# The last batch's norm ahead of the sum before it, and two spare products behind its transposition

## The chip, the cores and the metric

The kernel runs on one core of one Trainium2 chip. A core has five engines with a queue of instructions each: PE multiplies matrices (a weight load, PEld in the profile, and then a MATMUL that streams the other operand past the weights), DVE and ACT do elementwise work, POOL does elementwise work and starts some transfers, and SP starts transfers. Each engine takes its own instructions strictly in the order in which the program lists them and waits on semaphores for the others. PE writes its results to PSUM, of which this kernel uses eight banks; everything else lies in SBUF. The metric is the device time of one execution in microseconds (us). PE's clock can be halved for a while by the chip; the profile shows the share that was granted as PEclk.

## The reference, cut to what matters

Four stages follow one another on an input of 16 batches, each 256 by 256 in 32-bit floats: a per-batch expert adapter with a layer norm, an attention block with 16 heads and a feed-forward part, a conditional branch of small dense layers that ends in a layer norm, and one step of a stencil scheme. The change touches only the seam between the last two:

```python
y = x + out
mu = jnp.mean(y, axis=-1, keepdims=True)
var = jnp.mean((y - mu) ** 2, axis=-1, keepdims=True)
f = (y - mu) * jax.lax.rsqrt(var + EPS) * gamma + beta

Af = A_grid[None] * f[:, None]
Bf = B_grid[None] * f[:, None]
gradv_Af = _grad(Af[:, 0], 1) + _grad(Af[:, 1], 2)
gradvv_Bf = _grad2(Bf[:, 0], 1) + _grad2(Bf[:, 1], 2) \
    + _grad(_grad(Bf[:, 2], 2), 1) + _grad(_grad(Bf[:, 2], 1), 2)
df = -gradv_Af + gradvv_Bf * 0.5
out = jnp.maximum(f + df * dt[:, None, None], 0.0)
```

`_grad` and `_grad2` are first and second differences along one axis, with one-sided forms at the borders. All arithmetic is in 32-bit floats.

## The kernel before, in words

A batch is held as two chunks (`c`, or `k` where it is the contracted side) of 128 rows by 256 columns. Every stage of the chain is a Python generator over the 16 batches (`adapt`, `prepare`, `project`, `weigh`, `attend`, `enter`, `feed`, `end`, `step`). While the program is written, a planner, `Flow`, holds an estimated clock for each engine and picks which generator goes on next: the one with the earliest due time among those whose inputs are ready by the estimate. `flow.pe(1.6)` and the like advance these estimates; they emit nothing. What comes out is one fixed order of instructions for each engine. PSUM banks come from the planner too: `misc` takes the bank that was released longest ago by the estimates, of seven, and `free` gives it back.

So the batches overlap nearly everywhere: while one batch is in the stencil step, PE has attention or feed-forward work of the next. Only at the very end is there nothing to fill in. Just before its last sum the step of batch 14 (`b == B - 2`, line 1124) waits until the branch of batch 15 is written out; from there on the step is the only generator left, so that the end of batch 14's step and the whole step of batch 15 stand alone in program order.

The norm that ends the branch stage is split. `take_stats` (lines 413 to 426, called for the branch at line 1081) computes mean and variance on DVE and then 1/sqrt on POOL: `rs` in lines 421 and 422, and `nb` in lines 424 and 425. The step of a batch then begins with `normalized_affine` (line 443). For batches 0 to 14 it does the multiplication by gamma and the addition of beta on POOL. For batch 15 its `hurry` form is taken: four DVE instructions, chunk by chunk, lines 447 and 450. Line 447 needs the mean only, line 450 needs `rs`. The result overwrites `y` and is called `f`.

The step of one batch, in the order of the code:

- line 1102: four transposes of `f` on PE into a PSUM tile `e_t` (line 464 in the helper);
- line 1105: three DVE products of the transposed `f` with grids: `b2_`, `a1`, `b1_`, shown by the profile as e_b, e_a and e_b;
- lines 1109 and 1110: two POOL products of `f` with grids, `a0` and `b0`;
- lines 1116 and 1117: eight matmuls into `e_z`, which need `b2_` only; line 1121: DVE adds `e_z` to `a0`;
- lines 1133, 1149, 1139 and 1133 again: 32 matmuls into `e_d`: four with `b0`, sixteen with `a1` and `b1_`, eight narrow ones of 32 by 32 at the seam of the chunks, and four with `a0`;
- line 1165: DVE computes `o = e_d * dt + f`, for batch 15 in two halves; line 1169: ACT takes the maximum with zero; line 1171: SP starts the store.

The tiles of the step rotate through eight buffers, and a batch takes seven of them in the order `tmp`, `b2_`, `a1`, `b1_`, `a0`, `b0`, `o`.

Of the kernel before, what the change touches and what calls it, by code (L numbers as in the profile page):

```python
# [19 lines left out]
P = 128  # L20
B, S, D = 16, 256, 256
NC = S // P
# [148 lines left out]
def chain_kernel(ctx: ExitStack, tc: tile.TileContext, t: dict, out: bass.AP):  # L171
    nc = tc.nc
    ctx.enter_context(tc.manual_schedule())
    BANKS = 7
    flow = Flow(BANKS)
# [4 lines left out]
    def fixed(name, shape, dtype=F32, pool=const):  # L180
        return pool.tile(shape, dtype, name=name, tag=name)
# [14 lines left out]
    def misc(name, shape):  # L196
        numbers[name] = n = flow.take()
        return pp.tile(shape, F32, name=name, tag=f"m{n}")

    def free(name, at):  # L200

        flow.free_at[numbers.pop(name)] = at
        return at
# [67 lines left out]
    ident = fixed("ident", [P, P])  # L271
# [135 lines left out]
    b2, ln3_g, ln3_b = (rows_b[:, i * D : (i + 1) * D] for i in range(3))  # L407
    dt = rows_b[:, 3 * D :]
    w1_sr, w2_sr = w_sr[:, :NC, :], w_sr[:, NC:, :]
    a0_g, a1_g, b0_g, b1_g, b2_g, g_m, h_m = (grids[:, :, i * S : (i + 1) * S] for i in range(7))  # L410
# [17 lines left out]
    def normalized(dst, src, stat, first=False):  # L428
        mv, rs, nb = stat

        if first or max(flow.clock["DVE"], flow.clock["POOL"]) <= flow.clock["ACT"] + 0.3:
            for c in range(NC):
                nc.vector.tensor_scalar(
                    dst[:, c, :], src[:, c, :], mv[:, c, 0:1], rs[:, c : c + 1], ALU.subtract, ALU.mult
                )
            return flow.dve(0.65, flow.clock["POOL"])
        for c in range(NC):
            nc.scalar.activation(
                dst[:, c, :], src[:, c, :], AF.Identity, bias=nb[:, c : c + 1], scale=rs[:, c : c + 1]
            )  # L440
        return flow.act(0.97)

    def normalized_affine(dst, src, stat, gamma, beta, tmp, hurry=False):
        if hurry:
            mv, rs, _ = stat
            for c in range(NC):
                nc.vector.scalar_tensor_tensor(  # L447
                    tmp[:, c, :], src[:, c, :], mv[:, c, 0:1], gamma, ALU.subtract, ALU.mult
                )
                nc.vector.scalar_tensor_tensor(  # L450
                    dst[:, c, :], tmp[:, c, :], rs[:, c : c + 1], beta, ALU.mult, ALU.add
                )
            return flow.dve(2.1)
        at = normalized(tmp, src, stat)
        both = [P, NC, D]
        nc.gpsimd.tensor_tensor(tmp, tmp, gamma.unsqueeze(1).to_broadcast(both), ALU.mult)
        nc.gpsimd.tensor_tensor(dst, tmp, beta.unsqueeze(1).to_broadcast(both), ALU.add)
        return flow.pool(2.7, at)

    def transposed(ps, src):  # L460

        for k in range(NC):
            for c in range(NC):
                nc.tensor.transpose(  # L464
                    ps[:, k, c * P : (c + 1) * P], src[:, c, k * P : (k + 1) * P], ident
                )
        return flow.pe(0.44)
# [13 lines left out]
    ready, ys, stats2, lns, hts, stats3 = {}, {}, {}, {}, {}, {}  # L481
# [605 lines left out]
    def step():  # L1087
        def wide(name):
            return hp.tile([P, NC, S], F32, name=name, tag="g", bufs=8)

        yield lambda: ("branch", 0) in done
        for g in (a0_g, a1_g):
            nc.gpsimd.tensor_scalar(g, g, -1.0, None, ALU.mult)
        for b in range(B):
            yield lambda: ("branch", b) in done
            y, stat, at = stats3.pop(b)
            yield at, 0
            tmp = wide(f"e_tmp{b}")
            f = y
            yield normalized_affine(f, y, stat, ln3_g, ln3_b, tmp, b == B - 1)  # L1100
            ps_t = misc(f"e_t{b}", [P, NC, S])
            at = transposed(ps_t, f)
            b2_, a1, b1_ = (wide(f"e_{n}{b}") for n in ("b2", "a1", "b1"))
            for dst, grid in ((b2_, b2_g), (a1, a1_g), (b1_, b1_g)):
                nc.vector.tensor_tensor(dst, ps_t, grid, ALU.mult)  # L1105
                at = flow.dve(0.6, at)
            free(f"e_t{b}", at)
            a0, b0 = wide(f"e_a0{b}"), wide(f"e_b0{b}")
            nc.gpsimd.tensor_tensor(a0, f, a0_g, ALU.mult)
            nc.gpsimd.tensor_tensor(b0, f, b0_g, ALU.mult)  # L1110
            flow.pool(2.7)
            yield at - 1.4
            ps_z = misc(f"e_z{b}", [P, NC, S])
            for c in range(NC):
                rng = slice(c * P, (c + 1) * P)
                nc.tensor.matmul(ps_z[:, c, :], b2_[:, 0, rng], g_m[:, 0, :], start=True, stop=False)  # L1116
                nc.tensor.matmul(  # L1117
                    ps_z[:, c, reach[1]], b2_[:, 1, rng], g_m[:, 1, reach[1]], start=False, stop=True
                )
            at = flow.pe(1.35)  # L1120
            nc.vector.tensor_tensor(a0, ps_z, a0, ALU.add)
            at_z = free(f"e_z{b}", flow.dve(0.61, at))
            yield 0.0
            if b == B - 2:
                yield lambda: ("branch", B - 1) in done
            o = wide(f"e_o{b}")
            ps_d = misc(f"e_d{b}", [P, NC, S])

            def own(w, src, c, start=False, stop=False):
                rng = slice(c * P, (c + 1) * P)
                nc.tensor.matmul(ps_d[:, c, :], w[:, c, rng], src[:, c, :], start=start, stop=stop)  # L1133

            def next_to(w, src, c):
                near, far = slice(0, 32), slice(P - 32, P)
                at, of = (near, far) if c else (far, near)
                rng = slice(c * P + at.start, c * P + at.stop)
                nc.tensor.matmul(  # L1139
                    ps_d[at, c, :], w[of, 1 - c, rng], src[of, 1 - c, :], start=False, stop=False  # L1140
                )

            for c in range(NC):
                own(h_m, b0, c, start=c == 0)
            for c in range(NC):
                rng = slice(c * P, (c + 1) * P)
                for k in range(NC):
                    for src, w in ((a1, g_m), (b1_, h_m)):
                        nc.tensor.matmul(  # L1149
                            ps_d[:, c, reach[k]],  # L1150
                            src[:, k, rng],
                            w[:, k, reach[k]],
                            start=False,
                            stop=False,
                        )
            flow.pe(2.65)
            yield at_z
            for w, src in ((h_m, b0), (g_m, a0)):
                for c in range(NC):
                    next_to(w, src, c)  # L1160
            for c in range(NC):
                own(g_m, a0, c, stop=c == NC - 1)
            at = flow.pe(1.6)
            for part in [slice(c, c + 1) for c in range(NC)] if b == B - 1 else [slice(0, NC)]:
                nc.vector.scalar_tensor_tensor(  # L1165
                    o[:, part, :], ps_d[:, part, :], dt[:, b : b + 1], f[:, part, :], ALU.mult, ALU.add
                )
                at = flow.dve(0.75, at)
                nc.scalar.activation(o[:, part, :], o[:, part, :], AF.Relu)  # L1169
                flow.act(0.54, at)  # L1170
                nc.sync.dma_start(out=out[b].rearrange("(c p) d -> p c d", p=P)[:, part, :], in_=o[:, part, :])
            free(f"e_d{b}", at)
            done.add(("step", b))
# [7 lines left out]
    flow.add(feed(), 2.55, 13.9)  # L1181
    flow.add(end(), 3.08, 3.95)
    flow.add(step(), 4.65, 7.0)
    flow.run()

# [80 lines left out]
```

## Time and profile before

| what | value |
|---|---|
| time, median of 3 runs | 912.29 us (911.93 to 915.16) |
| the profiled execution's own time | 912.22 us |
| its span, first to last instruction shown | 910.4 us |
| PE busy in the span | 869.3 us (95%) |
| DVE, ACT, POOL busy | 636.2, 544.1, 377.4 us |
| mean granted PE clock | 0.99 |
| last matmul of batch 14 ends | 892.86 us |
| last matmul of the kernel ends | 906.24 us |

The profile is one execution, with times from the span's start. A row of its timeline gives a start, a length (from the first start to the last end if several instructions are merged), the engine, the source line, the operation with output and inputs, how many, and in square brackets how long the engine had been idle before and which instruction's end released it. A row of its windows gives, for a stretch of time, each engine's busy time with the number of instructions, then the granted PE clock, the busy share of the transfer engines and GB/s. Ends of matmuls are modelled, and times on POOL are rough.

### The profile page before, as it was taken

The numbers are of one execution on the slowest core, as the hardware profiler recorded it, in microseconds if no ns is written. First come the engines' busy times: TensorE is split into PE (matmuls) and PEld (weight loads), VectorE is DVE, ScalarE is ACT, GpSimd is POOL, SyncE is SP. The second block draws the span as 40 slices with busy tenths as digits, with TensorE's granted clock in tenths as the row PEclk, the third lists the DMA queues.
The fourth block names the chain that finished last, engine by engine and source line by source line (L and its number), as shares of the span: only waits on it lengthen the run. The fifth ranks groups of instructions, "written<-read, shape, count | busy, mean of one in ns | idle before, by whom it ended". The sixth has DMA issues, their size and how long they took to land. (4 is left out here: it accounts for less than half of the span.)

```text
span 910.4 us, 18249 instructions
## 1 busy us (share of the span) xinstructions
PE 869.3 (95%) x6184; PEld 668.7 (73%) x6184; DVE 636.2 (70%) x2087; ACT 544.1 (60%) x1537; POOL 377.4 (41%) x514
## 2 busy tenths in 40 slices
PE   7889998999999999999999999999999999999996
PEld 3557676777878777676877777787778778776875
DVE  5677867778777867757758686866768676767443
ACT  2576857576664767557765665847557474756230
POOL 3353455445416353351627245542446332422231
PEclk9999999999999999999999999999999999999998
DMA  8599977777888668778478777765857776670000
GB/s 274 166 267 316 285 166 191 183 200 191 203 204 201 179 166 221 217 185 209 125 191 222 179 193 175 190 166 161 195 152 181 180 203 173 176 190 31 13 30 23
DMA packets 130973, 163.25 MB, mean 179 GB/s; under 512 B 12714, under 2 KB 94780, under 8 KB 130876
## 3 DMA queue, kind: packets, MB, share of 16 engines
q0 software_dynamic: 31680, 62.92, 34.0%
q1 hardware_dynamic: 97920, 96.92, 33.5%
q10 hardware_dynamic: 1275, 2.19, 0.7%
q8 instruction: 52, 0.85, 0.4%
q14 instruction: 46, 0.37, 0.1%
HBM read 94.89 MB, written 4.19 MB: 109 GB/s over the span
## 5 line engine op out<-in xcount | busy, mean ns | idle before, releaser
L769 ACT ACTIVATE c_pr<-c_sc,c_mx 128x256 f32<-128x256 f32 x512 | 255.2, 500 | 207.5 <-DVE c_mx L758 203.9
L758 DVE CUSTOM_DVE_ANT_0 c_sc<-c_s,side 128x256 f32<-128x256 f32 x512 | 193.8, 417 | 35.7 <-PE c_s L740 20.2
L472 DVE COPY c_pts<-c_pt 128x512 f32<-128x512 f32 x206 | 137.0, 683 | 21.8 <-PE c_pt L464 21.2
L464 PE MATMUL c_pt<-ident,c_pr 128*128 128x128 f32 x1024 | 144.7, 278 | 7.4 <-ACT c_pr L769 3.6
L464 PEld LDWEIGHTS c_pt<-ident,c_pr 128*128 128x128 f32 x1024 | 114.3, 141 | 43.3 <-issue 14.5
L421 POOL TENSOR_SCALAR rs<-mv 128x2 f32<-128x2 f32 x64 | 14.2, 222 | 279.7 <-DVE mv L418 278.9
L924 PE MATMUL d_f<-d_ht,w 128*128 128x256 f32 x512 | 122.9, 383 | 4.0 <-DVE c_mx L758 2.2
L954 PE MATMUL d_o<-w,d_z 128*128 128x256 f32 x512 | 116.3, 381 | 0.1
L517 POOL DMA_DIRECT2D side<-neg x60 | 82.2, 1379 | 76.6 <-DMA side<-in_side 48.9
L924 PEld LDWEIGHTS d_f<-d_ht,w 128*128 128x128 f32 x512 | 92.7, 190 | 18.7 <-DVE c_mx L758 3.7
L954 PEld LDWEIGHTS d_o<-w,d_z 128*128 128x128 f32 x512 | 94.9, 190 | 14.5 <-issue 1.9
L769 ACT ACTIVATION_READ_ACCUMULATOR c_pr<-c_sc,c_mx 128x1 f32 x512 | 96.2, 188 | 0.0
L740 PE MATMUL c_s<-c_kt,c_qz 32*128 32x256 f32 x1024 | 77.6, 401 | 4.8 <-DVE x L582 1.9
L823 PE MATMUL c_c<-c_pts,c_va 128*32 128x256 f32 x1024 | 74.1, 386 | 2.7 <-DVE c_pts L472 2.5
L740 PEld LDWEIGHTS c_s<-c_kt,c_qz 32*128 32x128 f32 x1024 | 48.9, 184 | 24.5 <-issue 9.7
L962 DVE SCALAR_TENSOR_TENSOR y<-d_o,y 128x256 f32<-128x256 f32 x32 | 13.6, 425 | 63.3 <-PE d_o L954 63.3
L823 PEld LDWEIGHTS c_c<-c_pts,c_va 128*32 128x32 f32 x1024 | 27.9, 109 | 36.9 <-issue 17.9
L943 ACT ACTIVATE d_f<-d_z 128x512 f32<-128x512 f32 x64 | 38.3, 598 | 27.0 <-DVE d_z L940 26.3
L940 DVE TENSOR_SCALAR d_z<-d_f,cols 128x256 f32<-128x256 f32 x94 | 41.0, 477 | 16.2 <-PE d_f L924 16.0
L422 POOL TENSOR_TENSOR rs<-rs,inv_sqrt 128x2 f32<-128x2 f32 x64 | 45.9, 717 | 5.3
L947 DVE SCALAR_TENSOR_TENSOR d_z<-d_f,d_z 128x512 f32<-128x512 f32 x64 | 43.4, 677 | 1.8 <-ACT d_f L943 1.8
L1029 POOL TENSOR_TENSOR y<-y,d_bout 128x256 f32<-128x256 f32 x32 | 23.6, 790 | 47.1 <-PE d_t L464 32.1
(156 smaller groups left out, 1539.7 us busy)
## 6 DMA issues: line engine op xcount, KB each, us to landing
side<-in_side SPq DMA_DIRECT2D x256, 256.0 KB, 5.3
side<-neg POOLq DMA_DIRECT2D x60, 1024.0 KB, 8.1
d_w<-in_W_branch SPq DMA_DIRECT2D x16, 512.0 KB, 4.4
xt<-in_x_t SPq DMA_DIRECT2D x16, 256.0 KB, 6.1
x<-in_x SPq DMA_DIRECT2D x16, 256.0 KB, 5.9
out<-e_o SPq DMA_DIRECT2D x15, 256.0 KB, 3.7
w<-in_W SPq DMA_DIRECT2D x2, 1024.0 KB, 7.5
d_bout<-in_bl_branch SPq DMA_DIRECT2D x16, 128.0 KB, 4.5
```

The costliest lines, as they stand in the source:

```text
L422: nc.gpsimd.tensor_tensor(rs, rs, inv_sqrt, ALU.pow)
L464: nc.tensor.transpose(ps[:, k, c * P : (c + 1) * P], src[:, c, k * P : (k + 1) * P], ident)
L472: nc.vector.tensor_copy(dst, ps)
L517: nc.gpsimd.dma_start(out=sides[m].rearrange("p (h c) k -> p h (c k)", h=HB), in_=negs[m // 4].rearrange("p c k -> p (c k)").unsqueeze(1). ...
L740: nc.tensor.matmul(ps[i][:, c, :], qz[rows32, par, half, c * P : (c + 1) * P], k_t[rows32, half, :], start=b > 0, stop=b > 0 or c == NC - 1,)
L758: nc.vector.tensor_tensor_reduce(out=sc[:, c, :], in0=ps[i][:, c, :], in1=sb[:, i * NC + c, :], scale=-1.0, scalar=3.0e38, op0=ALU.add, op ...
L769: nc.scalar.activation(pr[:, c, :], sc[:, c, :], AF.Exp, bias=mx[:, c : c + 1], scale=-1.0, accum_out=sums[:, c, h : h + 1],)
L823: nc.tensor.matmul(ps_c[32 * i : 32 * i + 32, :], va[:, k, 4 * half + i, 2 * par : 2 * par + 2, :].rearrange("p e d -> p (e d)"), turned[i ...
L924: nc.tensor.matmul(ps_f[:, i, :], w1[:, k, f * P : (f + 1) * P], h_t[:, k, :], start=k == 0, stop=k == NC - 1,)
L940: nc.vector.tensor_scalar(z[:, i, :], ps_f[:, i, :], b1[:, f : f + 1], None, ALU.add)
L947: nc.vector.scalar_tensor_tensor(z, ps_f, 1.0, z, ALU.add, ALU.mult)
L954: nc.tensor.matmul(ps_o, us[f // 2][:, f % 2, c * P : (c + 1) * P], w2[:, f, :], start=f == 0, stop=f == NF - 1,)
```

## The change

For batch 15 the call of `normalized_affine` in its `hurry` form moves. It stood at the head of that batch's step; now it stands in the step of batch 14, behind that step's last matmuls and ahead of its DVE sum of line 1165. The four DVE instructions are the same. The head of batch 15's step only takes up the result. Its `tmp` tile is still requested between batch 14's `o` and batch 15's `b2_`, so every buffer's place in the rotation stays. Behind batch 15's four transposes, two matmuls are added: the identity as weights against 256 columns of a grid that has been in SBUF for long, into a PSUM bank taken for them that nobody reads. Other batches are written as before.

```diff
+        last = []
+
+        def awake(*columns):
+
+            ps = misc("awake", [P, NC * S])
+            for n in columns:
+                nc.tensor.matmul(ps[:, :n], ident, b2_g[:, 0, :n], start=True, stop=True)
+            free("awake", flow.clock["PE"])
+
         yield lambda: ("branch", 0) in done
         for g in (a0_g, a1_g):
             nc.gpsimd.tensor_scalar(g, g, -1.0, None, ALU.mult)
         for b in range(B):
             yield lambda: ("branch", b) in done
-            y, stat, at = stats3.pop(b)
-            yield at, 0
-            tmp = wide(f"e_tmp{b}")
-            f = y
-            yield normalized_affine(f, y, stat, ln3_g, ln3_b, tmp, b == B - 1)
+            if b < B - 1:
+                y, stat, at = stats3.pop(b)
+                yield at, 0
+                yield normalized_affine(y, y, stat, ln3_g, ln3_b, wide(f"e_tmp{b}"))
+                f = y
+            else:
+                f, at = last.pop()
+                yield at
             ps_t = misc(f"e_t{b}", [P, NC, S])
             at = transposed(ps_t, f)
+            if b == B - 1:
+                awake(256, 256)
...
             for c in range(NC):
                 own(g_m, a0, c, stop=c == NC - 1)
             at = flow.pe(1.6)
+            if b == B - 2:
+                y, stat, at_y = stats3.pop(B - 1)
+                last.append(
+                    (y, normalized_affine(y, y, stat, ln3_g, ln3_b, wide(f"e_tmp{B - 1}"), True))
+                )
             for part in [slice(c, c + 1) for c in range(NC)] if b == B - 1 else [slice(0, NC)]:
                 nc.vector.scalar_tensor_tensor(
                     o[:, part, :], ps_d[:, part, :], dt[:, b : b + 1], f[:, part, :], ALU.mult, ALU.add
```

## The prediction

> **What bounds the kernel now.** First the page's head: over the span PE is the busy engine.
>
> ```profile
> span 910.4 us, 18249 instructions
> PE 869.3 (95%) x6184; PEld 668.7 (73%) x6184; DVE 636.2 (70%) x2087; ACT 544.1 (60%) x1537; POOL 377.4 (41%) x514
> ```
>
> But the change touches only the last 20 us, and there the bound must be read anew. The view for that is the chain that ended last, in order of time (start, length, what):
>
> ```profile
> 891.78 1.07 PE e_d L1133 x4
> 892.88 0.75 DVE e_o L1165
> 893.64 0.40 DVE e_tmp L447
> 895.59 0.56 PE e_t L464 x3
> 896.18 0.70 DVE e_b L1105
> 896.92 1.22 PE e_z L1116 x2
> 905.16 1.07 PE e_d L1133 x4
> ```
>
> From the end of batch 14's last matmul (892.86) the end is set by batch 15 alone: sum, norm, transposition, product on DVE, and then PE without a break to 906.24. For 4.06 us PE has only four transposes. What releases what is in the timeline of the same stretch (start, length, engine, line):
>
> ```profile
> 889.98 0.18 DVE L418 BATCH_NORM_AGGREGATE mv<-st 128x2 f32<-128x6 f32 x1
> 890.55 0.71 POOL L422 TENSOR_TENSOR rs<-rs,inv_sqrt 128x2 f32<-128x2 f32 x1
> 892.88 0.75 DVE L1165 SCALAR_TENSOR_TENSOR e_o<-e_d,rows_b,y 128x512 f32<-128x512 f32 x1 [2.72 <-PE e_d L1133]
> 893.55 0.48 DVE L447 SCALAR_TENSOR_TENSOR e_tmp<-y,mv,rows_b 128x256 f32<-128x256 f32 x1
> 895.05 0.48 DVE L450 SCALAR_TENSOR_TENSOR y<-e_tmp,rs,rows_b 128x256 f32<-128x256 f32 x1
> 896.91 1.26 POOL L1110 TENSOR_TENSOR e_b<-y,grids 128x512 f32<-128x512 f32 x1
> ```
>
> The statistics are complete on POOL at 891.26, and DVE stands idle for 2.72 us up to 892.88, in front of a sum that waits for PE; the norm stands behind that sum.
>
> Last the windows, for the clock (after the first pair of numbers PE's busy time; the granted clock is the third number from the right). Up to the last matmul the clock changes only at 15.69, 19.10, 36.17, 39.58, 66.89, 70.30, 896.32 and 903.15, and the spaces between are whole multiples of 3.413 us (36.17 to 66.89 is 9 of them, 66.89 to 896.32 is 243): a grid, so I asked for the windows of that grid:
>
> ```profile
> 12.28:15.69 3.41, 2.19 (x21) 1.78 (x18) 2.02 (x8) 1.21 (x2) 1.84 (x2) 1.00 1.01 373
> 882.67:886.08 3.41, 1.99 (x8) 1.44 (x8) 0.21 (x1) 1.31 (x3) 1.22 (x2) 1.00 0.00 0
> 892.91:896.32 3.41, 0.85 (x4) 0.45 (x4) 2.63 (x6) 0.63 (x1) 0.64 (x1) 1.00 0.21 77
> 896.32:899.73 3.41, 2.81 (x9) 2.45 (x10) 1.74 (x3) 0.00 (x0) 1.85 (x2) 0.50 0.00 0
> 899.73:903.15 3.42, 3.42 (x14) 3.06 (x14) 0.69 (x1) 0.00 (x0) 0.00 (x0) 0.50 0.00 0
> ```
>
> The window with only the four transposes is followed by half clock; the next, with 2.81 busy, does not lift it; the full one after it does, at 903.15. So the gap costs twice: its length, and a stretch of 6.83 us at half speed behind it.
>
> **Part 1, the norm's new place.** Nothing is removed: four DVE instructions move ahead of one. No transfer is among them, and SP's and POOL's orders stay. The first (L447) needs the mean, there at 890.16. The second (L450) needs rs at 891.26, so I start it at 891.32. The next three distances are those of before (0.40, 0.52, and 0.48 for the last one's length): 891.72, 892.24, done at 892.72. New is that batch 14's sum, its ReLU and its store, and the three products of batch 15 now queue behind a wait for POOL. The sum waits for PE until 892.86 anyway, so that wait is covered by 0.14 us; beyond that each us of lateness of rs is a us on the path. The buffers asked for: tmp takes the one of batch 13's output, whose store was issued some 40 us before. I cost this at nothing.
>
> **Part 2, where the stall goes.** The last three transposes take 0.55 us; with y ready at 892.72 plus the 0.06 of before they run from 892.78 to 893.33. Late next is DVE: the sum stays at 892.88, and the instruction behind it started 0.67 later in the trace, at 893.55. So the first product (L1105) starts at 893.57 instead of 896.18, and e_z, 0.74 behind it as before, at 894.31 instead of 896.92: **2.61 us**. That is more than the norm's own 1.98, because the transposes also go under the sum. After e_z comes b0 from POOL: L1109 starts 0.15 after y (892.87), L1110 1.23 later, ends 895.36; PE wants it at 895.70. Spare 0.34, no cost; both multiply in the company of DVE before as after.
>
> **Part 3, the two spare matmuls.** No row shows them; the nearest is L1133 with the same 128x256 (four in 1.07, the last with its drain: 0.21 each). Two are 0.43, from 893.35 to 893.78 plus a drain of some 0.2, in front of an instruction that waits until 894.31. Cost between 0 and 0.43, the latter if transposes came 0.5 late; below zero not by time, only by the clock. I take 0. Their bank is the one released longest ago in the plan, not the e_d of batch 14 that is still being read.
>
> **Part 4, the clock.** Between 892.86 and 894.31 PE now has the transposes and 0.43 of full-width products; every window of 3.41 us that holds this stretch is otherwise full, so it has at least 3.41 - 1.45 + 0.43 = 2.39 us of dense matmuls. The window of 882.67, with eight such matmuls and 1.99 busy, kept full clock. The 2.19 of the window from 12.28, which lost it, is mostly sixteen products of 16 columns and says little of dense ones. So I expect full clock to the end. The work from e_z on then costs what batch 14's did: e_z from 880.61 to 881.92, the next group's start, 1.31, plus 0.08 for the first after a wait; e_d from 887.99 to 892.86, 4.87. Together 6.26 against 9.32 (896.92 to 906.24): **3.06 us**.
>
> Here the Trainium skill has a rule that speaks against my sum ("TensorE: Matmul & The Clock Gate", Part 1): the window runs free and does not restart with the kernel. The row agrees as to the grid (243 windows without drift), but one trace cannot show another phase. By the row, 3.06 are saved. By the rule, the stretch at half clock lies differently in each run of before. If the clock falls just after 896.92, the window behind is full, it lasts 3.41 and costs 1.7; if it falls before that, two windows may be needed, 2.3 to 3.3. The sum would then be anywhere from 4.3 to 5.9. The same page's Part 4 says that transpose mode does not count as PE being busy; the 892.91 window, which had nothing but transposes, fits, and I counted none above.
>
> **Sum.** Last matmul 894.31 + 6.26 = 900.57 instead of 906.24. The tail behind it stays: half sums, ReLU, store, 4.16 to the span's end, and 1.82 outside it. 912.22 - 2.61 - 3.06 = 906.55 for the profiled execution; the median of 912.29 stands 0.07 above it: 906.6. Because this trace's phase is near the dear end of what the clock can cost, I set 0.2 back: **906.8 us**.
>
> **The rivals.** (a) *The clock falls all the same*, because the products with the identity and the short gap are not enough. For it: the 2.19 window. Against: the 1.99 one. Only the 2.61 remain: 909.7. (b) *The start of e_z does not move that far*: POOL's products come late, since POOL's times are rough. For it: b0 is needed 2.6 us sooner and L1110 has 0.34 spare. If they take 1.5 longer, some 1.2 are lost, and 908 stands. (c) *Slower*: line 450 waits for rs ahead of batch 14's sum, with every later DVE instruction behind. The price is a us for each us that POOL ends after about 891.4; from 5.7 late the gain is gone, from 10.3 late it is 0.5% slower, 917. The row gives POOL nothing else in these 8 us, so this is hardly more than a formality. (d) *The change does not do what it says*: the first norm instruction is held until PE is through with batch 14 by a buffer or a wait that before's trace can't show, and nothing moves; 912.3. Against it: the tmp buffer is long free, and y has no reader left.
>
> **How the numbers follow.** About 0.5% (4.6 us) is what a measurement of this kernel can tell from no change. Full clock and moved start together: 0.86, own range 905.6 to 908; of these 0.70 are beyond 907.7 downwards, 0.16 are runs in which the half clock had cost before less than 2 us. (a) 0.07, (b) 0.02, (d) 0.02, all same; (c) 0.03. So faster 0.70, same 0.27, slower 0.03. The range is 905.6 to 909.9: from the largest sum with some early half-clock stretches shorter, to case (a).
>
> **What would show it.** Right: L447 near 890.2, L450's last end before 892.9, batch 14's L1165 still directly behind PE's last matmul; first L1105 some 0.7 behind that; e_z less than 1.6 behind batch 14's last matmul; two matmuls into the new bank between; granted clock 1.00 in all windows after it; from e_z to the last matmul about 6.3. Wrong: a clock of 0.50 after e_z, a wait of L1133 for POOL's L1110, or L1165 of batch 14 released by L450 and not by PE. The forecast fails most easily by the phase: if before's median runs had paid only 1.7 for the clock, 908 comes out with every step right.

## The result, and the profile after

The changed kernel took 907.80 us in the median of 6 runs (906.92 to 909.53), beside 912.13 (910.42 to 915.16) for the kernel before. The ratio is 0.9943 with a 95% interval of 0.9924 to 0.9962, 5.2 us or 0.57% faster (from 3.5 to 6.9 us). The ratio is an estimate over the single executions and not the quotient of the two medians, which lie 4.3 us apart. On another chip, beside other runs, the same kernel gave 907.76 and 0.9945 (0.9927 to 0.9964). The profiled execution took 907.62 us, with a span of 905.8.

Its timeline around the end of batch 14 (start, length, engine, line, in brackets the idle time before and its releaser; the change has moved lines 1105, 1116, 1133 and 1165 to 1119, 1130, 1147 and 1184):

```profile
891.15 0.45 DVE L447 SCALAR_TENSOR_TENSOR e_tmp<-y,mv,rows_b 128x256 f32<-128x256 f32 x1
891.32 0.36 POOL L421 TENSOR_SCALAR rs<-mv 128x2 f32<-128x2 f32 x1 [6.35 <-DVE mv L418]
891.76 0.71 POOL L422 TENSOR_TENSOR rs<-rs,inv_sqrt 128x2 f32<-128x2 f32 x1
892.51 0.51 DVE L450 SCALAR_TENSOR_TENSOR y<-e_tmp,rs,rows_b 128x256 f32<-128x256 f32 x1 [0.91 <-POOL rs L422]
893.45 0.48 DVE L450 SCALAR_TENSOR_TENSOR y<-e_tmp,rs,rows_b 128x256 f32<-128x256 f32 x1
893.75 0.79 PE L464 MATMUL e_t<-ident,y 128*128 128x128 f32 x4
893.96 0.75 DVE L1184 SCALAR_TENSOR_TENSOR e_o<-e_d,rows_b,y 128x512 f32<-128x512 f32 x1
894.37 1.03 PE L1097 MATMUL awake<-grids,ident 128*128 128x256 f32 x4
894.62 0.68 DVE L1119 TENSOR_TENSOR e_b<-e_t,grids 128x512 f32<-128x512 f32 x1
895.31 1.27 POOL L1124 TENSOR_TENSOR e_b<-y,grids 128x512 f32<-128x512 f32 x1
895.36 0.70 PE L1130 MATMUL e_z<-grids,e_b 128*128 128x256 f32 x2
```

The norm now runs while PE still works on batch 14, whose last matmul ends at 893.91 here. The transposes follow it at once, the sum of batch 14 runs beside them, and e_z starts 1.45 behind batch 14's last matmul, where it had been 4.06. In the windows of the clock's grid (in this execution its edges lie at 893.90 and every 3.413 us from there; PE's busy time is the second number, the granted clock the third from the right) the stretch that had lost the clock is full:

```profile
890.49:893.90 3.41, 3.41 (x26) 2.37 (x24) 2.40 (x7) 0.00 (x0) 1.54 (x4) 1.00 0.00 0
893.90:897.31 3.41, 3.41 (x20) 2.76 (x19) 2.85 (x6) 0.63 (x1) 2.50 (x2) 1.00 0.22 77
897.31:900.73 3.42, 3.42 (x28) 2.63 (x27) 0.42 (x1) 0.00 (x0) 0.00 (x0) 1.00 0.00 0
```

The chain that ended last, in order of time, has no DVE row left between the two batches. Its first e_d row behind e_z took 1.71 before (the first row here is from before) and takes 0.86 now:

```profile
899.86 1.71 PE e_d L1133 x4
```

```profile
893.92 0.62 PE e_t L464 x4
894.54 0.86 PE awake L1097 x4
895.40 0.65 PE e_z L1130 x2
896.93 0.86 PE e_d L1147 x4
900.57 1.07 PE e_d L1147 x4
```

The last matmul ends at 901.63, 6.27 behind e_z's start.

### The profile page after: what moved, and what is told of

Same layout as the page of the kernel before. It is cut to its first block, busy times and chain, and to the rows that moved or that the text cites. A ratio compares the mean times of both kernels' runs of the same rounds, so it can differ in the third digit from the quotient of the medians.

```text
span 905.8 us, 18259 instructions
## 1 busy us (share of the span) xinstructions
PE 867.4 (96%) x6188; PEld 668.2 (74%) x6188; DVE 636.7 (70%) x2087; ACT 544.1 (60%) x1537; POOL 377.6 (42%) x514
## 5 line engine op out<-in xcount | busy, mean ns | idle before, releaser
L421 POOL TENSOR_SCALAR rs<-mv 128x2 f32<-128x2 f32 x64 | 14.4, 224 | 281.4 <-DVE mv L418 280.5
L962 DVE SCALAR_TENSOR_TENSOR y<-d_o,y 128x256 f32<-128x256 f32 x32 | 13.6, 425 | 63.3 <-PE d_o L954 63.3
L947 DVE SCALAR_TENSOR_TENSOR d_z<-d_f,d_z 128x512 f32<-128x512 f32 x64 | 43.4, 678 | 1.8 <-ACT d_f L943 1.8
```

What stands on the lines that cost most here:

```text
L947: nc.vector.scalar_tensor_tensor(z, ps_f, 1.0, z, ALU.add, ALU.mult)
```

## The experiments

Two theories stood against each other on the clock: that the shorter gap alone keeps it, or that the two spare products do. A third question was whether rs is now what everything waits for, and what is left of the gap. The times beside each other were taken on one chip; "before" is the median of the kernel before there.

| run | median us | before | ratio (95% interval) |
|---|---|---|---|
| norm_alone | 908.42 | 913.12 | 0.9949 (0.9929 to 0.9969) |
| products_alone | 912.18 | 913.12 | 0.9981 (0.9967 to 0.9995) |
| products_filled | 910.68 | 913.12 | 0.9970 (0.9959 to 0.9981) |
| rs_late | 910.62 | 913.12 | 0.9980 (0.9971 to 0.9990) |
| after_again | 907.76 | 912.79 | 0.9945 (0.9927 to 0.9964) |
| late_one | 908.23 | 912.79 | 0.9939 (0.9916 to 0.9963) |
| late_one_bare | 909.94 | 912.79 | 0.9965 (0.9955 to 0.9974) |
| sooner | 907.48 | 912.79 | 0.9937 (0.9922 to 0.9953) |
| sooner_packed | 907.16 | 912.67 | 0.9934 (0.9913 to 0.9956) |

The medians hide most of what there is to see, because executions differ by several us before the end begins. So each profile is also cut at the start of batch 15's d_y matmuls (886.16 in before), the last point that all kernels share. "Half clock" adds up (1 - clock) x 2 x length over windows of 2 us ahead of that point; the last columns are distances in us from batch 14's last matmul to e_z, from e_z to the last matmul, and from d_y to the end of the span. They are taken from the ends as the profile holds them, and can differ by 0.02 from what its rounded rows give; the span is read to 0.1.

| profile of | d_y starts | half clock before it | gap to e_z | e_z to last | d_y to span end |
|---|---|---|---|---|---|
| before | 886.16 | 10.3 | 4.08 | 9.30 | 24.24 |
| before_look | 886.09 | 10.2 | 4.08 | 9.24 | 24.21 |
| after | 887.23 | 13.6 | 1.44 | 6.27 | 18.57 |
| after_again | 886.47 | 6.8 | 1.44 | 6.27 | 18.63 |
| norm_alone | 890.81 | 23.8 | 1.44 | 6.27 | 18.59 |
| norm_alone_b | 890.46 | 17.1 | 1.44 | 6.27 | 18.64 |
| norm_alone_c | 892.05 | 20.4 | 1.44 | 6.27 | 18.65 |
| products_alone | 886.75 | 13.6 | 4.94 | 6.90 | 22.75 |
| products_filled | 890.11 | 17.0 | 4.07 | 6.27 | 21.29 |
| rs_late | 886.16 | 10.2 | 4.23 | 7.37 | 22.54 |
| late_one | 887.40 | 17.0 | 2.50 | 6.28 | 19.70 |
| late_one_bare | 890.61 | 23.8 | 2.50 | 6.28 | 19.69 |
| sooner | 887.03 | 10.3 | none | 7.44 | 18.57 |
| sooner_packed | 890.23 | 17.1 | none | 6.27 | 17.57 |

The last column repeats within 0.1 us for one kernel; the first differs by 6 us over these executions, and mostly grows with the half clock ahead of it.

**The norm alone.** The change without its spare products:

```diff
-            if b == B - 1:
-                awake(256, 256)
```

> The norm is moved as in the change, the two spare products are left out. Behind batch 14's last matmul PE then has only four transposes in about 1.45 us before e_z, the rest of every 3.41 us window is dense. Theory (the moved norm does it, and the gap is now too short for the clock to fall): e_z still 1.45 behind batch 14's last matmul, granted clock 1.00 from there on, 6.3 us from e_z to the last matmul, time as with the whole change, 907.8 within 0.5. Rival (the spare products hold the clock): the same 1.45, but a clock of 0.50 behind it and 8 to 9.5 us from e_z to the last matmul, 909.5 to 911.

> The moved norm without the spare products, for another phase. Theory (a gap of 1.45 us is short enough in any phase): e_z to the last matmul 6.27 at full clock. Rival (the spare products are needed in some phases): a clock of 0.50 behind e_z and 7.5 to 9.5 us, in at least one of the two looks.

> The same once more, for a third phase: 6.27 us at full clock by the theory, 7.5 to 9.5 by the rival.

All three traces gave 1.44 and 6.27 at full clock, and from d_y to the span's end 18.59 to 18.65, where the change has 18.57 and 18.63. The median, 908.42, lies within its noise of the whole change. So in these traces the norm's new place does by itself all that the change does, the clock included. The chain of the third has DVE's product in the place of the spare ones, and e_z starts no earlier and no later:

```profile
898.78 0.75 DVE e_o L1175
899.53 0.61 DVE e_b L1110
900.18 0.70 PE e_z L1121 x2
```

The grid's edges, counted from d_y, lay nearly alike in the three traces (d_y at 0.67 to 0.72 of a window), so they are not three phases. In the third, the window that holds most of the gap was this:

```profile
896.60:900.01 3.41, 2.76 (x17) 1.49 (x16) 2.63 (x5) 0.45 (x1) 2.26 (x4) 1.00 0.00 0
```

Of the 1.44 us PE idles 0.81, so that no phase can leave a window with less than 2.6. In these traces the spare products neither saved nor cost anything. That they do nothing in any other phase is argued from the 2.6, not shown: with d_y at 0.05 of a window, as in the first trace of the change, the whole gap lies in one window, and the norm alone was not traced there. Nor is busy time by itself a sure measure. In products_filled the window from 14.05, mostly products of 16 columns, lost the clock with 2.56 busy, and in after_again the one from 30.89 kept it with 1.59.

**The products alone.** The norm stays in its old place, the two spare products are added behind the transposes:

```diff
             at = transposed(ps_t, f)
+            if b == B - 1:
+                awake(256, 256)
```

> The norm stays where it was before, the two spare products alone are added behind the transposes of batch 15. They run in a wait of 0.8 us and take 0.86 (four MATMUL records of 0.21 for two calls, as the trace after shows). Theory: the gap behind batch 14's last matmul stays at 4.06 us, a 3.41 us window in it has at most some 1.4 us of matmuls, the clock falls all the same; time as before, 912.1 within 0.7, e_z at most 0.1 later. Rival (the products are what lifts the clock): e_z 4.1 behind batch 14's last matmul as before, but full clock and 6.3 us from there, 909.0 to 909.8.

Its timeline:

```profile
896.66 1.91 PE L1095 MATMUL awake<-grids,ident 128*128 128x256 f32 x4
896.91 0.69 DVE L1114 TENSOR_TENSOR e_b<-e_t,grids 128x512 f32<-128x512 f32 x1 [0.79 <-PE e_t L464]
898.37 1.06 PE L1125 MATMUL e_z<-grids,e_b 128*128 128x256 f32 x2
```

The clock had fallen at 896.44, ahead of the products, so they took 1.91 instead of 1.03, and e_z waited for them: the gap is 4.94, not the "at most 0.1 later" that was expected. On the other hand they filled the window 896.44 to 899.85 (3.41 busy), and the clock came back after one window, not two: e_z to last 6.90. Together 1.5 us less than before in this trace. The median says 0.2% with an interval that ends just short of 1, below what counts as a change here. Both theories missed this mixture. In this trace the products alone did not keep the clock; other phases of the grid were not met.

**The clock alone.** The norm in its old place, and PE's waits filled with spare products:

```diff
+            if b == B - 1:
+                awake(256, 256, 256, 256)
...
-            at = transposed(ps_t, f)
+            at = transposed(ps_t, f, (lambda: awake(256)) if b == B - 1 else None)
+            if b == B - 1:
+                awake(256, 256)
```

The function handed to `transposed` is called between the first transpose and the second.

> The norm stays where it was before; the waits of PE between batch 14's last matmul and batch 15's e_z are filled with spare products: four calls (1.72 us) ahead of the transposes, one (0.43) between the first and the second transpose, two (0.86) behind them. This takes away the fall of the clock alone. Theory: e_z stays 4.06 to 4.2 behind batch 14's last matmul, granted clock 1.00, 6.3 us from e_z to the last matmul; saves what the clock costs, on average over the phase of the grid 2.3, at most 3.3: 909.0 to 910.4. Rival (the clock costs nothing on the median run, the norm's place is all): 912 within 0.5.

The gap stayed 4.07, and e_z to last went to 6.27 at full clock; d_y to the span's end is 2.95 shorter than in before. The ratio 0.9970 says 2.7 us (1.7 to 3.8), the medians 2.4. So of the change's 5.2 (5.67 in the traces) the clock by itself is worth about 2.7 (2.95), and the rest is the shorter gap.

**rs later.** The whole change, with two products of 128x512 on POOL ahead of batch 15's power:

```diff
+        if name == f"3_{B - 1}":
...
+            for _ in range(2):
+                nc.gpsimd.tensor_tensor(spare, b0_g, b1_g, ALU.mult)
         nc.gpsimd.tensor_tensor(rs, rs, inv_sqrt, ALU.pow)
```

> The whole change, with two extra products of 128x512 on POOL (1.27 us each by the neighbouring rows) ahead of the power that gives rs of batch 15; they go into a buffer that nobody reads any more. Theory: rs is on the path with no slack left, so the norm, the sum of batch 14, the transposes and e_z come 2.5 us later, and e_z stands 3.9 to 4.0 behind batch 14's last matmul. Of that gap PE has 1.5 us of work, so the clock falls in part of the runs: 907.8 plus 2.5 if it stays, plus 4 to 5.5 if it falls, 910.3 to 913. Rival (rs had slack, the sum of batch 14 or the transposes end last): less than 2.0 later, below 909.8.

The timeline and the window with the gap:

```profile
893.88 0.51 DVE L454 SCALAR_TENSOR_TENSOR y<-e_tmp,rs,rows_b 128x256 f32<-128x256 f32 x1 [3.34 <-POOL rs L426]
895.75 1.54 PE L1101 MATMUL awake<-grids,ident 128*128 128x256 f32 x4
897.08 1.06 PE L1134 MATMUL e_z<-grids,e_b 128*128 128x256 f32 x2
```

```profile
892.71:896.12 3.41, 1.20 (x7) 0.87 (x7) 2.21 (x5) 0.12 (x1) 2.26 (x5) 1.00 0.00 0
896.12:899.53 3.41, 3.41 (x12) 2.76 (x11) 1.71 (x3) 0.51 (x1) 1.83 (x2) 0.50 0.21 77
```

The gap is 4.23, a window with 1.20 busy cost the clock, and the whole is 4.0 longer from d_y than the change. The gap was expected at 3.9 to 4.0. The rest comes from the spare products: they took 1.54 here, most of it at half clock, and e_z waited for them, since the DVE product that it reads was done at 896.64. The median is 2.9 above that of the change on another chip, within what was expected. rs had no slack left.

**One late, with and without the products.** The same with one POOL product, once on the whole change, once on the norm alone.

> The whole change with one extra POOL product (1.27 us) ahead of the power of batch 15, so that the gap from batch 14's last matmul to e_z is some 2.7 us with four transposes and the two spare products in it. Theory (the clock goes by how much PE worked in a window of 3.41 us, and rows of 1.7 to 2.0 us held it): the window has some 1.6 us of matmuls and 0.6 of transposes, at the edge; full clock in the trace if it holds, and then 1.3 behind the change, 909; up to 3 more if it falls. Rival (spare products do nothing for the clock): same times with and without them.

> The same gap of some 2.7 us without the spare products: in it PE has four transposes only, so a window of 3.41 us that holds the gap has 0.7 us of matmuls. Theory: the clock falls to 0.50 behind the gap in nearly all phases, e_z to the last matmul takes 8 to 9.5 us in the trace, 1.7 to 3.3 slower than with the spare products, 911 to 912.5. Rival (the gap is still too short for the clock to fall, spare products or not): 6.3 us, 909.

Both gave a gap of 2.50, 1.06 longer than the change, and both kept full clock in the profile. Without the products it was this:

```profile
895.10:898.52 3.42, 2.55 (x16) 1.23 (x14) 1.50 (x4) 0.00 (x0) 2.32 (x4) 1.00 0.00 0
898.52:901.93 3.41, 2.63 (x15) 2.21 (x16) 2.87 (x5) 0.63 (x1) 2.50 (x2) 1.00 0.22 77
```

An edge of the grid cuts the gap in two, and each window keeps over 2.5 us of work. The expectation that the clock falls "in nearly all phases" without the products failed in this trace, and its median, 909.94, is below the 911 that was expected. By the ratios late_one_bare is slower than late_one by 0.26% of 912.8, 2.4 us (1.7 by the medians), with intervals that just overlap. That would fit a clock that the products hold in part of the runs at this longer gap, but the profile of late_one_bare also had 6.8 us more of half clock far ahead of the end than that of late_one. What the products do at 2.5 us stays open. Nor do the medians show late_one's longer gap: with four executions its 0.9939 is no higher than the 0.9945 of the change, though the trace has 1.1 us more from d_y to the end.

**What is left of the gap.** A version that goes on from the norm alone. Its core:

```diff
+            nc.vector.tensor_scalar(rs, mv[:, :, 1], EPS, None, ALU.add)
+            nc.gpsimd.tensor_tensor(rs, rs, inv_sqrt, ALU.pow)
...
             for c in range(NC):
                 nc.vector.scalar_tensor_tensor(
                     tmp[:, c, :], src[:, c, :], mv[:, c, 0:1], gamma, ALU.subtract, ALU.mult
                 )
+            for c in range(NC):
                 nc.vector.scalar_tensor_tensor(
                     dst[:, c, :], tmp[:, c, :], rs[:, c : c + 1], beta, ALU.mult, ALU.add
                 )
...
+                    heads.append(turned_grids(B - 1, y))
                 for c in range(NC):
                     own(g_m, a0, c, stop=c == NC - 1)
...
+            if b == B - 1:
+                for c in range(NC):
+                    for w, src in ((h_m, b0), (g_m, a0)):
+                        next_to(w, src, c)
+                    own(g_m, a0, c, stop=True)
```

`turned_grids` holds the transposes and the three products of line 1105; for batch 15 it now stands ahead of batch 14's last four MATMUL records.

> A version that goes on from the change, without spare products. For batch 15: epsilon is added on DVE, so that POOL has only the power to do; the two L447 instructions go ahead of the two L450 and fill the wait for it; the four transposes and the three DVE products go ahead of the last four MATMUL records of batch 14 and of its sum, so that these records fill PE's wait for the first product; the last e_d is in two tiles, chunk 0 ends before chunk 1's last products, and its sum, ReLU and store go under them. Theory (the rest of the gap is the power, the transposes and the first product in a row): y ready 0.9 us sooner, e_z about 0.6 behind batch 14's last matmul where it was 1.45, the tail behind the last matmul 0.4 shorter, full clock: 1.2 us below the change. Rival (POOL's b0 for batch 15, which waits for batch 14's last matmul, ends last): PE waits ahead of the e_d products, 0.4 to 0.6 below the change.

> The changed kernel as it is, on the chip of the runs beside it, to be compared with them and as a second look at another phase of the clock's grid. Both theories (spare products needed or not): e_z 1.45 behind batch 14's last matmul, full clock, 6.3 us from e_z to the last matmul, 0.5 to 0.65% below before.

e_z now follows batch 14's last matmul without a gap, 7.45 behind d_y where the change has 8.13, so 0.68 sooner. But nothing was gained: from d_y to the span's end 18.57, as the change. The rival's wait for POOL's b0 was not there either. The chain shows where it went: the narrow matmuls of line 1155 stand in it twice,

```profile
898.71 0.97 PE e_d L1155 x4
900.32 0.97 PE e_d L1155 x4
```

for 0.97 each, where eight together take 0.98. That is 0.96 of the 1.17 by which e_z to last has grown. The second version keeps these eight together and parts only the last two products and the sums:

```diff
+            for w, src in ((h_m, b0), (g_m, a0)):
+                for c in range(NC):
+                    next_to(w, src, c)
...
+            for c in range(NC):
+                own(g_m, a0, c, stop=c == NC - 1 or b == B - 1)
```

> As the version called sooner, but the eight narrow products of batch 15 stay together, four on b0 and then four on a0 over both chunks, as in the kernel before; only the last two products and the sums are by chunk. Theory (the narrow ones of different chunks run side by side in the array, and to pull them apart took 0.97 us twice instead of 0.98 once): from batch 15's d_y to the last matmul 13.6 to 13.8 us, where the change has 14.40 and sooner 14.89, and the tail 0.4 shorter: 1.1 below the change, 906.6 where it has 907.8. Rival (the lost 1.2 us of sooner came from e_z's own start, too early for POOL's b0): 14.4 or more.

Its chain and its last rows of the timeline:

```profile
901.91 0.98 PE e_d L1155 x8
```

```profile
902.82 1.13 PE L1149 MATMUL e_d<-e_a,grids 128*128 128x256 f32 x4
903.56 0.91 DVE L1186 SCALAR_TENSOR_TENSOR e_o<-e_d,rows_b,y 128x256 f32<-128x256 f32 x2 [3.48 <-PE e_d L1149]
```

From d_y to the last matmul 13.72 (the change: 14.40), and the first half of the sum starts at 903.56 while the last matmul still runs to 903.95. From d_y to the span's end it is 17.57, 1.0 below the change, as the theory had it. In the medians it is 907.16 beside 907.76 of the change, 0.07%, with intervals that lie over each other: better in the trace, not shown to be better in time. The row of 0.98 shows that the order of the narrow products was what sooner had lost.

**The kernel before once more.**

> The kernel before, for another phase of the clock's grid. Theory (the cost of the fall depends on where the grid's edges lie): 14's last matmul to e_z 4.1 again, but e_z to the last matmul between 8.0 and 9.6 us, where one trace had 9.30. Rival (the fall costs the same each time): 9.3.

It gave 9.24, with the clock's fall at 896.16, only 0.16 earlier than in the first trace. So the two traces of before agree, but mostly because they met nearly the same phase.

## Why the prediction was right, step by step

The forecast was 906.8 with a range of 905.6 to 909.9 and the likeliest case a moved start with full clock; 907.80 came, and the case was that one.

*Part 1, the norm's new place.* "I cost this at nothing" held, though the cover of 0.14 was used up. Counted from d_y, y was to be ready at 6.56; it was at 6.70, and batch 14's last matmul ends at 6.68. So by 0.02 the sum of batch 14 waited for the norm and not for PE, a sign that the prediction had named for being wrong; it is too small to show in the end. What was missed is that the first norm instruction now lies on DVE beside POOL's L421. That one took 0.36 in all eight profiles with the norm in its new place and line 421 unchanged, and 0.22 in before, before_look, products_alone and products_filled, where DVE was idle. It ends 0.08 after L447 does. The trace of before already had such a pair, near its start, from another norm:

```profile
15.67 0.45 DVE L447 SCALAR_TENSOR_TENSOR b_tmp<-x,mv,rows_a 128x256 f32<-128x256 f32 x1
15.83 0.37 POOL L421 TENSOR_SCALAR rs<-mv 128x2 f32<-128x2 f32 x1 [1.63 <-DVE mv L418]
```

The Trainium skill has a rule that fits ("SBUF — State Buffer", section "SBUF: two separate sides"): DVE and POOL share a pair of ports as an exclusive lock, which a DVE instruction with two SBUF inputs holds to its end. L447 reads y and gamma from SBUF. No run changed L447's inputs, but nine times in before L421 ran beside L947, a DVE instruction that takes one of its two inputs from PSUM, and took 0.22 each time. The rule is not the whole account: L424 begins 0.04 after L450, which has two SBUF inputs too, and takes its usual 0.20. The prediction called POOL's order unchanged and so took its times as unchanged.

*Part 2, where the stall goes.* The first product starts 0.71 behind batch 14's last matmul, e_z 1.45 behind it: 0.71 and 1.45 were forecast. The 2.61 is measured as 4.08 less 1.44, 2.64. POOL's L1124 ended at 896.58, and the matmuls that read it started at 896.77, 0.19 spare instead of 0.34.

*Part 3, the spare products.* Their cost of nothing was right, their size wrong by half: two products of the program are four MATMUL records, 0.86 us, not 0.43. The full-width f32 products of the step stand in the profile as two records each; the row that was used as the nearest shows it ("four in 1.07" for two products), and I counted records as products. At 0.86 they end just when e_z's input is ready (895.36), so they were within a tenth of a us of costing something; that the nothing held in spite of the wrong size was luck. As to their use, the three traces of norm_alone show none.

*Part 4, the clock.* Full clock to the end, and 6.27 from e_z instead of the forecast 6.26, against 9.30: 3.03 in the trace. The count of PE's work that led there was too low: it left the transposes out, on the word of a page that it names, and the trace of before decides against that. In its window from 462.84 PE was busy throughout, for 2.62 us with transposes of line 464, so that only 0.80 is left without them; the clock stayed at 1.00, and did so until 896.32:

```profile
462.84:466.26 3.42, 3.42 (x32) 2.76 (x25) 2.45 (x7) 1.89 (x9) 0.00 (x0) 1.00 0.71 174
```

The window of 892.91 with nothing but transposes had 0.85 of work at most, and so decides nothing. The warning that this is not the same in each run is half shown. Over the executions the edges of the grid lie differently against the span (falls at 36.17, 37.15, 36.44 and, for products_filled, 31.11 are not whole windows of 3.413 apart), and the stretch behind e_z was two windows in the two traces of before and one in products_alone and rs_late. In the timed executions the clock came to 2.7 by the ratio and 2.4 by the medians (products_filled), between the 1.7 and the 3.3 of the estimate.

*The sum.* From d_y to the span's end before less after is 24.24 - 18.57 = 5.67, and 5.67 was the sum. That the profiled execution took 907.62 and not 906.55 lies ahead of the change: batch 15's d_y began at 887.23 instead of 886.16, 1.07 later, after 13.6 us of half clock instead of 10.3. The trace that the sum was made against had nearly the earliest d_y of the fourteen. So the 0.2 that was set back for the phase was the right thought on the wrong term: what varies most is not the clock at the end but the clock in the first fifth of the kernel. How much of the distance from the 5.67 of the traces to the 5.2 or 4.3 of the timed executions belongs to either is not shown.

*The rivals.* (a), the clock falls all the same, is refuted by all five traces with a gap of 1.44. (b), POOL too late, came to nothing. (c), rs on the path, is a true mechanism: 1.1 us of lateness gave 1.06 us of gap in late_one; only the lateness itself was 0.14 in the change. (d) is refuted by L447 at 891.15.

## What to carry to other kernels

A gap on PE can cost twice, its length and a stretch at half clock behind it, and the second part is read from the windows of the clock's own grid and not from the longest single wait (1.92 us in before, ahead of its first transpose). Work that moves onto an idle engine takes that idleness away from its neighbour, so a row of another engine at that place may no longer hold. And before a small gain is measured, cut the traces at the last point that both kernels share: here 5.67 us repeat to 0.1, while whole executions differ by 6.

## What the runs showed of the hardware that I had not expected

Narrow matmuls of 32 by 32 that lie in different rows and columns of the array run side by side when they are neighbours in the program: in sooner_packed, with both chunks next to each other, four records on e_b take 0.62 from first start to last end, and in sooner, one chunk at a time, two take 0.61. A POOL instruction on 128x2 elements takes 0.36 instead of 0.22, and the power 0.87 instead of 0.71, when it starts beside an L447 (L451 in sooner) with two operands in SBUF (L421 in after, L423 in sooner); L424 beside L450 does not. In the fourteen profiles d_y stands at only two places in a window of the grid, 0.02 to 0.17 or 0.66 to 0.72 of it, though the grid's place against the start of the span varies; why stays open. Transposes held the clock in before as other products do (2.62 of 3.42 us in the window from 462.84). And a window of 3.41 us with 2.55 of work kept the clock (late_one_bare) where one with 1.20 lost it (rs_late), so that a gap of 2.5 us can pass unpunished when an edge of the grid falls into it. No sharp threshold shows: 2.56 lost it in products_filled, 1.59 kept it in after_again.
